# Streamed weights begun ahead of their stage in a four-layer attention and feed-forward kernel

## The chip, the cores and the metric

One Trainium2 chip; the kernel runs on 1 of its cores. The metric is device time in microseconds, the median of 3 runs. A profiled execution gives the trace that all views come from. Engines are named as the profile names them: PE (TensorE, matrix multiply), PEld (its weight loads), DVE (VectorE), ACT (ScalarE), POOL (GpSimd) and SP (SyncE, which here issues nearly all transfers).

## The reference

Sixteen samples x of 256 x 128, each with a context of 1601 x 64, pass through four layers. Every layer is an attention of x over the context and a feed-forward part, each on a layer norm of x and added to x:

```
for l in 0..3:
    x = x + xattn_l(layernorm(x), context)
    x = x + ffn_l(layernorm(x))
```

- Layer 0: causal self-attention plus cross attention, 16 heads of 8; then a mixture of 32 small experts, top 4 (hidden size 1024 in all).
- Layer 1: cross attention, 16 heads of 8; then a convolution with ternary weights and quantised activations.
- Layer 2: two blocks with 16 heads of 32, the first over x itself, the second over the context. Each is attention, a projection (li1), and an inner feed-forward part (norm, li2, gelu, li3). Then 8 experts, top 1.
- Layer 3: cross attention, 16 heads of 8; then 16 experts, top 2, with a shared one (hidden size 1280 in all).

All is float32.

## The kernel before

**The order of work is written out by hand.** A schedule made while the program is built decides in which order each engine gets its instructions; engines then run in that order and wait on semaphores. Two samples ("lanes") are in work at a time. `seq` lists (sample, layer) pairs: both samples' layer 0, both samples' layer 1, and so on, then the next pair.

**The frame is the cross attention over 1601 keys.** It is cut into slabs of 4 heads, 4 slabs to an attention, 256 in all. A slab has 7 steps of two key tiles of 128: scores (`st_ops`, L447), exponentials (`exps`, L462), weighing of values one step later (`weigh`, L473). Beside slab i run the score maxima of slab i + 1 (`Slab.maxima`, L544: matmuls into `bank`, reduced by DVE at L552). After a slab's last step, `normalised` (L485) divides by the sums: for heads of 32 a reciprocal (L502) and a product (L503) on DVE.

**Everything else is coroutines.** `life(b)` (L1033) is a sample's whole path outside the frame; each `yield` in it ends a slot's share. After each step the frame calls `slot()` (L1073) twice, one directly after the other. A slot advances the key line or the value line in turn (keys and values of the coming attention), and then each sample's chain by one `yield`. So what two consecutive steps of a chain do is emitted into the engines' in-order streams with an attention step between them, or with none. When a chain asks for its attention (`attend`, L771) it stands still until its slabs are done. If the next slab's sample isn't that far, `until` (L1094) calls slots with no attention between them. That happens ahead of every l2 cross attention: 12 slots for each sample, and 25 at the very end.

**The chain of l2.** `l2_attn` (L960) calls `mha` (L905) twice. The first, pre `l2_a1`, attends to the sample itself: norm, transpose, `affine_T`, then q, k and v from the streamed `qkv` weights, then `own_attention` (L564). The second, pre `l2_a2`, is the cross attention. Both end alike: load the streamed `li` weights, first `down` (L759; 4 chunks of 128 and a bias row), norm, transpose, `hidden`, gelu, second `down`.

**Streamed weights.** Weights that don't fit for good come through `stream` (L263): a tile of 128 x 1536 from a pool of two buffers (`wst`), and one transfer issued by SP at L266. `ws_room`, a `Room(2)` (L59), counts the free buffers while the program is built: `take` yields until there is one. There are 8 streamed loads a sample: `s_l0f_0` and `_1` in `l0_ffn` (L810), `s_l2_a1_qkv`, `s_l2_a1_li` and `s_l2_a2_li` in `mha`, `s_l3f_0` to `_2` in `l3_ffn` (L997). Each is issued where its stage begins, followed by two or three empty yields.

**SP's queue** is in order too. Besides the streamed loads it holds the context, x, the output, and the spreads (`spread`, L407: 4 transfers for a slab, 16 for a tensor) that place queries and keys of heads of 8 in four row groups. A transfer into a buffer waits for the last reader of that buffer.

Of the kernel before, what the change touches and what calls it, by code (L numbers as in the profile page):

```python
# [20 lines left out]
P = 128  # L21
# [53 lines left out]
def model(ctx: ExitStack, tc: tile.TileContext, d, out):  # L75
# [187 lines left out]
    def stream(n, w):  # L263
# [2 lines left out]
        nc.sync.dma_start(out=t[:, :w], in_=d[n])  # L266
        return t

    def ln(src, tag="z"):

        st = sm.tile([P, 2, 6], F32, tag="st", name=name("st"))
        mv = sm.tile([P, 2, 2], F32, tag="mv", name=name("mv"))
        rs = sm.tile([P, 2], F32, tag="rs", name=name("rs"))
        for q in range(2):
            nc.vector.bn_stats(out=st[:, q, :], in_=src[:, q, :])  # L275
            nc.vector.bn_aggr(out=mv[:, q, :], in_=st[:, q, :])
        nc.vector.tensor_scalar(rs, mv[:, :, 1], EPS, None, ALU.add)  # L277
        nc.gpsimd.tensor_tensor(rs, rs, neghalf[:, 0:2], ALU.pow)  # L278
        yield
        z = tok(tag)  # L280
        for q in range(2):
            nc.vector.tensor_scalar(  # L282
                z[:, q, :], src[:, q, :], mv[:, q, 0:1], rs[:, q : q + 1], ALU.subtract, ALU.mult
            )
        return z
# [141 lines left out]
    class Att:  # L427
# [4 lines left out]
        def __init__(self, dims, q, nk):  # L432
            self.d8 = dims == 8
            self.q, self.nk = q, nk
            self.scale = S8 if self.d8 else S32
            self.k, self.v = {}, {}
            self.o = tok("o") if self.d8 else wide("oT")
            self.done = False

        def value(self, s, t, g, r):  # L440
            if self.nk == T:
# [366 lines left out]
        return residual(x, tok_out([(cols(yT), W["l0_Wp"]), bias_row(0)]))  # L808

    def l0_ffn(x):  # L810
        z = yield from ln(x)
        xz = tok("xz")
        nc.gpsimd.tensor_tensor(xz, x, z, ALU.add)
        zT = yield from to_T(z)
        p = bank()
        mm(p[:32, :T], W["l0f_hash"], zT)
        hT = chan("hT")[:32, :T]
        evac(hT, p[:32, :T])
        yield
        lg = wp.tile([P, 2, 32], F32, tag="lg32", name=name("lg"), bufs=1)  # L820
        evac(lg, tok_out([(cols(hT), W["l0f_keys"])], n=32))
        yield
        gate = wp.tile([P, 2, 32], F32, tag="gate32", name=name("gate"), bufs=1)
        yield from route(lg, 32, 4, gate)
        gT = yield from gates_T(gate, 32)
        o = xz
        for c0 in (0, 4):
            yield from ws_room.take()
            w = stream(f"s_l0f_{c0 // 4}", 1024)
            for _ in range(2):  # L830
                yield
            h = wide("h")
            s = flat(h)
            for i in (0, 512):
                nc.scalar.activation(s[:, i : i + 512], hidden(w, zT, i // T), AF.Silu)
            yield
            for i in (0, 512):
                nc.vector.tensor_tensor(s[:, i : i + 512], expanded(exp32, gT, c0 + i // T), s[:, i : i + 512], ALU.mult)
            yield
            p = down([h], w[:, 512:], 4)  # L840
            ws_room.give()
            n = tok("x")
            nc.vector.scalar_tensor_tensor(n, p, W["l0f_scale"], o, ALU.mult, ALU.add)
            o = n
        return o
# [58 lines left out]

    def mha(x1, pre, cross, r0):  # L905

        z = yield from ln(x1)
        yield
        pz = transposed(z)
        xT = affine_T(pz, pre + "_lnx_g", pre + "_lnx_b", "xT")  # L910
        if cross:
            yield
            q = yield from slabs(W[pre + "_wq"], xT, "q")
            att = Att(32, q, NK)
            yield from attend(att)
        else:
            yT = affine_T(pz, pre + "_lny_g", pre + "_lny_b", "yT")
            yield from own_room.take()
            yield from ws_room.take()
            w = stream("s_" + pre + "_qkv", 1536)  # L920
            for _ in range(3):
                yield
            q = yield from slabs(w[:, :512], xT, "q")
            k = yield from slabs(w[:, 512:1024], yT, "k")
            v = wide("v")
            for t in range(2):
                p = bank()
                mm(p, yT[:, t * P : (t + 1) * P], w[:, 1024:])
                evac(flat(v)[:, t * 512 : (t + 1) * 512], p)
                yield  # L930
            ws_room.give()
            att = Att(32, q, T)
            att.k = {s: k[:, s, :] for s in range(4)}
            att.v = {0: flat(v).rearrange("p (t h e) -> p t h e", t=2, h=H)}
            yield from own_attention(att, False, (ALU.is_gt, 1))
            own_room.give()
        o = att.o
        yield from ws_room.take()
        w = stream("s_" + pre + "_li", 1536)
        for _ in range(3):  # L940
            yield
        p = down([o], w, 4, [bias_row(r0)])
        xo = tok("xo")
        nc.vector.tensor_tensor(xo, p, x1, ALU.add)
        z = yield from ln(xo)
        yield
        zT = affine_T(transposed(z), pre + "_ln3_g", pre + "_ln3_b", "xT")
        yield
        h = wide("h")
        pr = [hidden(w[:, 512:1024], zT, c) for c in (0, 2)]  # L950
        for c in range(4):
            nc.scalar.activation(
                h[:, c, :], pr[c // 2][:, (c % 2) * T : (c % 2 + 1) * T], AF.Gelu, bias=W[pre + "_li2_b"][:, c : c + 1]
            )
        yield
        p = down([h], w[:, 1024:], 4, [bias_row(r0 + 1)])
        ws_room.give()
        return xo, p
# [36 lines left out]
        return residual(x, down([h], flat(W["l2f_W2"]), 2, [(cols(gT), W["l2f_b2"])]))  # L995

    def l3_ffn(x):  # L997
        z = yield from ln(x)
        zT = yield from to_T(z)
        lg = wp.tile([P, 2, 17], F32, tag="lg17", name=name("lg"), bufs=1)  # L1000
        evac(lg, tok_out([(cols(zT), W["l3f_Wg"])], n=17))
        yield
        gate = wp.tile([P, 2, 17], F32, tag="gate17", name=name("gate"), bufs=1)

        sg = sm.tile([P, 2], F32, tag="sg", name=name("sg"), bufs=1)
        nc.scalar.activation(sg, lg[:, :, 16], AF.Exp, scale=-1.0)
        yield from route(lg[:, :, :16], 16, 2, gate[:, :, :16])
        nc.vector.tensor_scalar(sg, sg, 1.0, None, ALU.add)
        nc.vector.reciprocal(gate[:, :, 16], sg)
        gT = yield from gates_T(gate, 17, 32)  # L1010
        for c0, n in ((0, 4), (4, 4), (8, 2)):
            yield from ws_room.take()
            w = stream(f"s_l3f_{c0 // 4}", 3 * n * P)
            for _ in range(2):
                yield
            h = wide("h")
            s = flat(h)
            for i in range(0, n * T, 512):
                nc.scalar.activation(s[:, i : i + 512], hidden(w, zT, i // T), AF.Silu)
            yield  # L1020
            for i in range(0, n * T, 512):
                o = s[:, i : i + 512]
                nc.vector.tensor_tensor(o, hidden(w[:, n * P :], zT, i // T), o, ALU.mult)
            yield
            for i in range(0, n * T, 512):
                o = s[:, i : i + 512]
                nc.vector.tensor_tensor(o, expanded(exp64, gT, c0 + i // T), o, ALU.mult)  # L1027
            yield
            x = residual(x, down([h], w[:, 2 * n * P :], n))
            ws_room.give()  # L1030
        return x
# [17 lines left out]
    ready = {}  # L1049
# [23 lines left out]
    def slot():  # L1073
        begin()
        if later:
            g = later.popleft()
            if advance(g)[0]:
                later.appendleft(g)
        for i, l in enumerate(lines):
            if i == turn[0] % 2:  # L1080
                advance(l)
        turn[0] += 1
        for c in list(chains):
            if c[0] is not None and c[0] in ready:
                if not ready[c[0]].done:
                    continue
                del ready[c[0]]
            alive, att = advance(c[1])
            if att is not None:
                ready[c[0]] = att  # L1090
            if not alive:
                chains.remove(c)
# [10 lines left out]
    def slab(i):  # L1103

        n, s = divmod(i, 4)
        if n >= len(seq):
            return None
        b = seq[n][0]
        until(lambda: b in ready and not ready[b].done and n in k_of and s in k_of[n])
        att = ready[b]  # L1110
        att.k, att.v = k_of[n], v_of.setdefault(n, {})
        slabs_of[i] = Slab(att, s, i % 2)
        return slabs_of[i]

# [8 lines left out]
    with tc.manual_schedule():  # L1123
# [28 lines left out]
        for i in range(4 * len(seq)):  # L1152
            nxt = slab(i + 1)
# [155 lines left out]
```

## Time and profile before

| | |
|---|---|
| median of 3 runs | 11254.35 us (11251.69 to 11277.46) |
| profiled execution, its own time | 11315.87 us |
| its span, first to last instruction | 11313.9 us |
| mean granted TensorE clock | 0.795 |
| busy: PE, DVE, ACT, POOL | 9940.3, 5942.1, 4978.6, 952.6 us |
| DMA queue q1 (SP's), share of 16 engines | 11.4% |
| li loads (`ws<-in_s_l_a_li_dram`) | 32 of 768.0 KB, 4.2 us to landing |
| l0f loads | 32 of 512.0 KB, 5.5 us |
| l3f loads | 32 of 768.0 KB, 6.7 us, and 16 of 384.0 KB |

A line of the timeline gives start, duration, engine, source line, operation, output<-inputs, shape and count; in brackets the idle time of that engine before it, and what ended it. A line of the waits gives who waited for whom, the sum in us, how often, and the longest. Most matrix operations stand under L172, the helper `mm`, so they are told apart by their tiles: `bank<-ws,oT` is the first down of an li stage, `bank<-xT,ws` its hidden layer (or q of the first l2 block), `bank<-ws,h` its second down; `mx<-k,q` are scores of an own attention; `nmp` and `nmT` carry the shift by the maxima. The durations of matmuls overlap, since PE is pipelined.

### The profile page before, as it was taken

What the parts mean: (1) busy time and instruction counts of PE and PEld (TensorE: products, weight loads), DVE (VectorE), ACT (ScalarE), POOL (GpSimd) and SP (SyncE); (2) the same over time, 40 slices, a digit from 0 to 9 for tenths busy, and PEclk for the clock granted to TensorE, in tenths of its full rate; (3) what the DMA queues carried; (4) which work ended last, traced back from release to release, by engine and by line L of the source; (5) the groups of instructions that cost most, each with busy time, mean ns of one, the idle gap of its engine ahead of it and who ended that gap; (6) DMA issues with size and microseconds to landing.
All of it is one profiled execution on the core that took longest, in us unless ns stands there. A gap on an engine that the chain in (4) does not pass through costs nothing.

```text
span 11313.9 us, 204909 instructions
## 1 busy us (share of the span) xinstructions
PE 9940.3 (88%) x86834; PEld 5384.7 (48%) x86874; DVE 5942.1 (53%) x13070; ACT 4978.6 (44%) x6812; POOL 952.6 (8%) x2283
## 2 busy tenths in 40 slices
PE   6989899898998979989798897988989989798898
PEld 3445444454444544445454454544544445454454
DVE  4544555445554455545555454554555545455455
ACT  3433454334543445434454344543444434444344
POOL 2000100001000010000100001000010000100000
PEclk7679777796777977789777896778977689777897
DMA  2100111001110011100111001110011100111011
GB/s 57 36 7 15 35 44 36 7 18 36 40 36 7 18 38 39 36 7 18 42 39 31 7 19 42 37 31 7 20 43 36 31 7 19 43 36 32 7 23 26
DMA packets 158827, 313.09 MB, mean 28 GB/s; under 512 B 65163, under 2 KB 116275, under 8 KB 157910
## 3 DMA queue, kind: packets, MB, share of 16 engines
q1 hardware_dynamic: 154676, 297.83, 11.4%
q8 instruction: 683, 11.19, 0.4%
q14 instruction: 234, 1.92, 0.1%
q0 software_dynamic: 768, 1.48, 0.0%
q10 hardware_dynamic: 2466, 0.68, 0.0%
HBM read 98.31 MB, written 2.10 MB: 9 GB/s over the span
## 4 chain that ended last, share of the span: by engine, by line
PE 73%; DVE 13%; ACT 5%; issue 4%; POOL 3%; SPq 2%; DMA 1%; DVEq 0%; POOLq 0%; ACTq 0%
PE bank L172 58%; PE st L172 10%; DVE mx L552 4%; ACT p L464 3%; DVE nm L579 2%; SPq L411 2%; PE mx L172 1%; PE bank L492 1%; PE bank L298 1%; POOL rs L278 1%; DVE z L282 1%; POOL p L603 1%; DVE st L275 1%; DVE hl L405 1%; ACT y L239 1%
## 5 line engine op out<-in xcount | busy, mean ns | idle before, releaser
L552 DVE TENSOR_REDUCE mx<-bank 128x1 f32<-128x400 f32 (+2 forms) x8192 | 4165.5, 568 | 2382.7 <-PE bank L172 2292.8
L464 ACT ACTIVATE p<-st 128x1024 f32<-128x1024 f32 (+1 forms) x3840 | 3500.6, 963 | 3735.0 <-PE st L172 2376.3
L172 PE MATMUL bank<-k,q 32*128 32x400 f32 (+2 forms) x10240 | 3663.6, 574 | 479.6 <-DVE mx L552 265.8
L172 PEld LDWEIGHTS bank<-k,q 32*128 32x128 f32 x10240 | 1653.0, 216 | 1900.6 <-DVE mx L552 1065.7
L172 PE MATMUL bank<-p,v 128*9 128x256 f32 (+3 forms) x27648 | 2483.3, 472 | 32.5 <-POOL p L603 32.5
L172 PE MATMUL st<-q,k 32*128 32x256 f32 (+1 forms) x18176 | 2011.0, 394 | 156.5 <-DVE nm L579 82.4
L172 PEld LDWEIGHTS st<-q,k 32*128 32x128 f32 (+1 forms) x18176 | 1313.4, 213 | 507.4 <-ACT p L464 174.3
L172 PE MATMUL st<-nmT,ones 32*128 32x512 bf16 (+1 forms) x7680 | 1291.8, 442 | 0.0
L172 PEld LDWEIGHTS bank<-p,v 128*9 128x9 f32 (+3 forms) x27648 | 688.0, 105 | 1243.6 <-issue 988.7
L172 PE MATMUL bank<-p,ones 128*32 128x256 f32 (+1 forms) x7680 | 611.3, 392 | 20.2 <-ACT p L464 20.2
L509 POOL CAST nmp<-nm 128x8 bf16<-128x8 f32 x384 | 83.7, 218 | 6017.6 <-DVE nm L558 4434.6
L579 DVE TENSOR_REDUCE nm<-mx 128x4 f32<-128x1024 f32 x256 | 301.7, 1221 | 317.2 <-PE mx L172 312.5
L172 PEld LDWEIGHTS <-ones 32*128 32x128 bf16 (+1 forms) x7680 | 410.2, 109 | 41.1
L278 POOL TENSOR_TENSOR rs<-rs,neghalf 128x2 f32<-128x2 f32 x240 | 167.6, 698 | 3002.5 <-DVE rs L277 3002.5
L239 ACT COPY v<-bank 128x512 f32<-128x512 f32 (+3 forms) x592 | 228.8, 449 | 372.2 <-PE bank L172 372.2
L172 PEld LDWEIGHTS bank<-p,ones 128*32 128x32 f32 (+1 forms) x7680 | 251.8, 113 | 217.2 <-ACT p L464 39.4
L603 POOL TENSOR_SCALAR_AFFINE_SELECT p<-p 128x1024 f32<-128x1024 f32 x256 | 266.6, 1063 | 841.6 <-PE bank L172 524.1
L502 DVE RECIPROCAL rc<-bank 128x256 f32<-128x256 f32 x128 | 224.7, 1756 | 175.4 <-PE bank L172 171.6
L172 PE MATMUL bank<-ws,h 128*128 128x128 f32 x1664 | 307.0, 351 | 3.2 <-DVE h L1027 0.8
L464 ACT ACT_TABLE_LOAD x141 | 180.9, 1283 | 262.0 <-PE st L172 139.1
L172 PEld LDWEIGHTS bank<-ws,h 128*128 128x128 f32 x1664 | 275.7, 255 | 38.6 <-DVE h L1027 12.5
L492 PE MATMUL bank<-ident,y 128*128 128x128 f32 x512 | 136.3, 360 | 155.1 <-ACT y L239 154.6
(240 smaller groups left out, 7258.1 us busy)
## 6 DMA issues: line engine op xcount, KB each, us to landing
k<-hl SPq DMA_DIRECT2D x768, 200.2 KB, 4.0
q<-hl SPq DMA_DIRECT2D x1024, 32.0 KB, 1.9
ws<-in_s_l_a_li_dram SPq DMA_DIRECT2D x32, 768.0 KB, 4.2
ws<-in_s_l3f_dram SPq DMA_DIRECT2D x32, 768.0 KB, 6.7
ws<-in_s_l0f_dram SPq DMA_DIRECT2D x32, 512.0 KB, 5.5
ws<-in_s_l_a_qkv_dram SPq DMA_DIRECT2D x16, 768.0 KB
k<-hl SPq DMA_DIRECT2D x256, 32.0 KB, 1.9
ws<-in_s_l3f_dram SPq DMA_DIRECT2D x16, 384.0 KB
```

What stands on the lines that cost most here:

```text
L172: nc.tensor.matmul(out=o, lhsT=l, rhs=r, start=start, stop=stop, skip_group_check=free)
L239: nc.scalar.copy(o, i)
L275: nc.vector.bn_stats(out=st[:, q, :], in_=src[:, q, :])
L278: nc.gpsimd.tensor_tensor(rs, rs, neghalf[:, 0:2], ALU.pow)
L282: nc.vector.tensor_scalar(z[:, q, :], src[:, q, :], mv[:, q, 0:1], rs[:, q : q + 1], ALU.subtract, ALU.mult)
L411: nc.sync.dma_start(out=raw(o)[r::4, :], in_=raw(hl[c])[32 * s : 32 * s + 32, :])
L464: nc.scalar.activation(e[:r, :, :n, :], sc[:r, :, :n, :], AF.Exp, scale=att.scale)
L492: nc.tensor.transpose(t[:, q * P : (q + 1) * P], y[:, q * P : (q + 1) * P], ident)
L502: nc.vector.reciprocal(rc, av[:, 1, :])
L552: nc.vector.tensor_reduce(self.mx[:, q, g, c : c + 1], p[:, : k1 - k0], AX.X, ALU.max)
L579: nc.vector.tensor_reduce(o, sc[hp], AX.X, ALU.max, negate=True)
L603: nc.gpsimd.affine_select(out=e, in_=e, pattern=[[0, 2], [sign * P, 2], [-sign, T]], compare_op=op, fill=0.0, base=0, channel_multiplier=sign,
```

## The change

A load is begun ahead of its stage if a buffer is free at that point; otherwise it is made at the stage as before, now with four empty yields. Where it was begun ahead, the stage has no empty yield. The points: at the norm of `l0_ffn`, `l3_ffn` and the first `mha`; one group ahead within `l0_ffn` and `l3_ffn`; after the v projection for the first `li`; and for the second `li` once the attention's last slab has had its maxima begun (`began` reaches 3). So that `mha` can watch `began`, a chain that waits for its attention is now advanced in every slot; it still goes on only when the attention is done.

```diff
+    def early(n, w):
+        if not ws_room.n:
+            return None
+        ws_room.n -= 1
+        return stream(n, w)
+
+    def arrived(t, n, w):
+        if t is None:
+            yield from ws_room.take()
+            t = stream(n, w)
+            for _ in range(4):
+                yield
+        return t
...
+            self.began = 0
...
     def l0_ffn(x):
+        nxt = early("s_l0f_0", 1024)
         z = yield from ln(x)
...
         for c0 in (0, 4):
-            yield from ws_room.take()
-            w = stream(f"s_l0f_{c0 // 4}", 1024)
-            for _ in range(2):
-                yield
+            w = yield from arrived(nxt, f"s_l0f_{c0 // 4}", 1024)
+            nxt = early("s_l0f_1", 1024) if c0 == 0 else None
...
     def mha(x1, pre, cross, r0):
+        nxt = None if cross else early("s_" + pre + "_qkv", 1536)
         z = yield from ln(x1)
...
-            yield from attend(att)
+            wait = attend(att)
+            yield next(wait)
+            while att.began < 3:
+                yield
+            nxt = early("s_" + pre + "_li", 1536)
+            yield from wait
         else:
...
-            yield from ws_room.take()
-            w = stream("s_" + pre + "_qkv", 1536)
-            for _ in range(3):
-                yield
+            w = yield from arrived(nxt, "s_" + pre + "_qkv", 1536)
...
             ws_room.give()
+            nxt = early("s_" + pre + "_li", 1536)
...
         o = att.o
-        yield from ws_room.take()
-        w = stream("s_" + pre + "_li", 1536)
-        for _ in range(3):
-            yield
+        w = yield from arrived(nxt, "s_" + pre + "_li", 1536)
...
     def l3_ffn(x):
+        nxt = early("s_l3f_0", 1536)
         z = yield from ln(x)
...
         for c0, n in ((0, 4), (4, 4), (8, 2)):
-            yield from ws_room.take()
-            w = stream(f"s_l3f_{c0 // 4}", 3 * n * P)
-            for _ in range(2):
-                yield
+            w = yield from arrived(nxt, f"s_l3f_{c0 // 4}", 3 * n * P)
+            nxt = early(f"s_l3f_{c0 // 4 + 1}", 768 if c0 else 1536) if c0 < 8 else None
...
         for c in list(chains):
-            if c[0] is not None and c[0] in ready:
-                if not ready[c[0]].done:
-                    continue
+            if c[0] in ready and ready[c[0]].done:
                 del ready[c[0]]
             alive, att = advance(c[1])
...
         att.k, att.v = k_of[n], v_of.setdefault(n, {})
+        att.began = s
```

## The prediction

> **What bounds the kernel now.** I read four views, from wide to narrow: the page, the PE's own waits, the timeline at the longest of them, and a table of stretches.
>
> The page first: the lines of busy time and of the chain.
>
> ```profile
> span 11313.9 us, 204909 instructions
> PE 9940.3 (88%) x86834; PEld 5384.7 (48%) x86874; DVE 5942.1 (53%) x13070; ACT 4978.6 (44%) x6812; POOL 952.6 (8%) x2283
> PE 73%; DVE 13%; ACT 5%; issue 4%; POOL 3%; SPq 2%; DMA 1%; DVEq 0%; POOLq 0%; ACTq 0%
> ```
>
> PE is busy for 88% and holds 73% of the chain; DMA holds 1%. Earlier loads can win only where PE stands still: at most 11313.9 - 9940.3 = 1374 us, and in fact only what of it hangs on the streamed weights. The PE's own waits say how much that is (us, times, longest):
>
> ```profile
> PE bank L172 <- DVE mx L552: 265.8, 316, 5.4
> PE bank L298 <- DVE z L282: 151.7, 39, 11.8
> PE bank L172 <- DMA ws<-in_s_l_a_li_dram: 81.0, 7, 13.4
> ```
>
> Only one stream is ever waited for: the li weights, 7 times, 81.0 us (0.7%). The l0f, l3f and qkv streams do not appear, so loading them earlier is worth nothing directly. The timeline at one of the seven, SP and then PE (start, duration):
>
> ```profile
> 3990.58 10.04 SPq L411 DMA_DIRECT2D q<-hl  x16
> 4000.72 13.90 SPq L411 DMA_DIRECT2D k<-hl  x20
> 4014.67 1.04 SPq L266 DMA_DIRECT2D ws<-in_s_l_a_li_dram  x1
> 4015.81 11.25 SPq L411 DMA_DIRECT2D q<-hl  x16
> ```
>
> ```profile
> 4007.91 0.48 PE L172 MATMUL bank<-rows,ones 1*128 1x128 f32 x2
> 4021.52 2.08 PE L172 MATMUL bank<-ws,oT 128*128 128x128 f32 x8 [13.12 <-DMA ws<-in_s_l_a_li_dram]
> ```
>
> The load isn't slow: 6.85 us from issue to use. It is issued late, behind 36 small spreads of about 0.65 us each in SP's order. This is the second sample of a pair in its second (cross) block, where the next pair's l0 spreads come in. The other 25 li loads are issued well ahead already, because SP runs ahead of PE.
>
> The second place is the gap ahead of the l2 cross attention. There the emission loop calls slots with no attention between them:
>
> ```profile
> 3519.51 1.05 PE L172 MATMUL bank<-p,v 128*9 128x256 f32 x16
> 3522.85 0.29 PE L172 MATMUL bank<-ident,nmp 128*128 128x128 bf16 x2 [2.29 <-POOL nmp L512]
> ...
> 3532.26 0.49 PE L298 MATMUL bank<-ident,z 128*128 128x128 f32 x2 [1.12 <-DVE z L282]
> 3533.41 2.76 PE L172 MATMUL bank<-xT,ws 128*128 128x256 f32 x8 [0.66 <-ACT xT L311]
> ...
> 3548.38 0.73 PE L298 MATMUL bank<-ident,z 128*128 128x128 f32 x2 [6.76 <-DVE z L282]
> 3549.77 3.78 PE L172 MATMUL bank<-xT,w_l_a_wq 128*128 128x256 f32 x8 [0.65 <-ACT xT L311]
> 3553.48 1.04 PE L172 MATMUL bank<-k,q 32*128 32x402 f32 x2
> ```
>
> From 3519.1 to 3553.5 PE does only the li chain: 34.4 us for a pair's first sample, 30.7 to 32.7 for its second.
>
> **The change part by part.** All sums are against the profiled execution (11315.87 us), which is 0.55% above the median of 11254.35.
>
> *What moves.* The slots can be counted from the loops before anything runs. The gap has 12 of them in each sample; with the change it has 6, since 3 yields go at qkv and 3 at li. All slots together go from 3825 to 3723: 16 x 6, and 6 at the end. No operation is added or removed. In the changed SP order, the second sample's last li load stands right behind an earlier l3 key spread, two slabs ahead of its use, and no longer behind the 36 spreads.
>
> *The li wait, 7 x 11.6 = 81.0 us.* It goes. What is late next: the next pair's own attention (mx<-k,q) needs k spreads that SP issues until 4014.6, and PE now arrives 13 us sooner. Its first score came at 4005.64, so slab 0 is there in time, and slabs 1 to 3 are issued by about 4011. Ends: 0 (the spreads take over the whole wait) and 81; I take 10 of each 11.6, so **-70**, since most of the spreads are already issued.
>
> *The clock after that wait.* The li matmuls took 4.80 us after the wait against 2.66 for the same group at full clock elsewhere. I take 2 us for each of the 7: **-14** (ends 0 and 28).
>
> *The gap.* Six slots fewer are not half of 34 us, and this is where I chose. The last two slots of the attention step before the gap were empty and are now filled with the hidden matmuls and second down, which nothing covers there either. Truly put under attention are the first down, its norm and the transpose: 3524.02 to 3533.41 = 9.4 us, plus the 2.29 us that PE waited for the shift (its reduction stood behind a 1.76 us reciprocal that now comes earlier). The same stretch in the second sample, at a higher clock, is 7.3 + 1.1. What is put under attention still costs PE its time: down 2.66, transpose 0.5, the key matmuls inside it 1.0 and a new in-order wait. Down now comes one slot after the last slab's division (1.76 + 0.42 us on DVE; 2.3 us from last weigh matmul to oT), with no attention between. A bias row, three of four chunks and sometimes a value tile come first, so 1.5 of it stays. Together 5.7; at half clock 2.5 more. First sample 11.7 - 7.2 = 4.5, second 8.4 - 5.7 = 2.7: 3.6 x 16 = **-58** (ends: 0, and half the gap, 16 x 16 = 260).
>
> *New in-order waits elsewhere.* PE takes matmuls in order, so the attention step behind pays. In the cross block, li's down now follows the division in the same slot: 1 us each for the nine without a DMA wait before, **+9** (ends 0 and 2.3 x 16 = 37). At qkv, q's matmuls follow the transpose in the same slot: ACT's xT costs 0.66 us in the row at 3533.41 and up to 2.6 behind an exponential pair of 1.94 us; 1.3 x 16 = **+21** (ends 10 and 42).
>
> *At nothing:* l0f and l3f loads (no row waits for them; cover: SP is slabs ahead; without it, 6.7 us a load); the tail, where the third l3f load waits for the first buffer as before and the 6 slots gone were empty; an early load behind a buffer still being read, which holds SP only until PE reaches that point, with the spreads emitted later behind it (without that, one slab's wait, 22 to 44 us).
>
> **A rule against the trace.** The rows first, of the gap and of the slab after it; the columns are stretch, its length, busy of PE, PEld, DVE, ACT, POOL, clock, DMA, GB/s.
>
> ```profile
> 3519.10:3553.50 34.40, 22.92 (x98) 15.29 (x97) 9.22 (x29) 7.90 (x15) 3.70 (x8) 0.62 0.07 24
> 3559.00:3595.00 36.00, 35.75 (x227) 16.93 (x231) 14.84 (x30) 11.23 (x14) 0.87 (x4) 0.50 0.00 1
> ```
>
> PE is busy for 35.75 of 36 us and the clock stays at 0.50. The Trainium skill (TensorE: Matmul & The Clock Gate, Part 1: The HAM clock gate) says the opposite: about 3.4 us of sustained activity brings full clock back. By the rule this slab would be at full clock after one window and no gain lies there. By the row, about 16 us are lost here in each pair (36 against some 20 at full clock), and a gap that ends otherwise could free 8 x 16 = 128 us, or put other slabs into that state. Nothing in the trace says which way it falls, so the sum has 0, and the range takes it in.
>
> Sum: -70 - 14 - 58 + 9 + 21 = -112 us of 11315.87, that is 11204 profiled; scaled by 0.995, 11254 - 111 = **11143 us** (-1.0%).
>
> **The rivals.**
> - *As summed* (0.56): 11090 to 11200.
> - *More than summed* (0.19): the gap really halves (-260 in place of -58), or the half-clock slab goes (-128). For it: the slab repeats in every pair behind this gap. Against it: half of the freed slots stand uncovered. About 11015 with the slab, 10940 with the gap.
> - *The wait only changes its name* (0.18): with the spreads still serial on SP, own attention or a bank waits for them in place of li, and of -84 only some 20 are left: 112 - 64 = 48, so 11206; with the gap's part gone too it is -20 + 30 = +10, 11264. For it: SP is busy without a break from 3990 to 4027, and PE stood 5 us at 3996.8 for other work of this knot. Most of it is within 0.3%.
> - *Slower* (0.07): the merged slots. At 48 places (32 downs, 16 qkv) PE now stands in order ahead of a short chain on DVE or ACT. Without these waits the gains are 81 + 14 + 58 + 24 (the 1.5 us taken off the gap) = 177; from 177 / 48 = 3.7 us a place the change loses. I take 1 to 1.5; with the whole 2.3 us and as much again until DVE's reductions (265.8 us waited for already) have caught up it is 4.6, so 48 x 4.6 - 177 = +44: 11298.
>
> **How the numbers follow.** A measurement of this kernel can tell about 0.3% (34 us) from no change. Below 11220 lie the first two cases and a part of the third: faster 0.79; same 0.15; slower 0.06. The range runs from the half-clock slab freed (11020) to the wait renamed with little left (11245).
>
> **What would show it.** Right: the li row is gone from PE's waits and no k or q row of like size comes; the last st matmul to the first maxima of the l2 attention falls from 34 and 31 us to some 23; new PE waits for oT (L503) and xT of 1 to 2 us. Wrong: a DMA k<-hl row of tens of us; a gap of 17 us (I underrated) or over 28; the slab behind the gap at a clock of 1.0, or other slabs fallen to 0.5; oT waits near 4 us.

## The result and the profile after

The changed kernel takes 11099.24 us (median of 4 executions, 11084.67 to 11147.29) against 11265.90 us of the kernel before on the same chip (11251.69 to 11295.38): ratio 0.9857, 95% interval [0.9825, 0.9888]. Set against the 11254 us of the prediction, that is -161 us where -111 was forecast; the forecast of 11143 us was 44 us too high (50 by the change itself: the kernel before was 12 us slower this time). The profiled execution took 11147.29 us at a mean granted clock of 0.803 (before: 11315.87 us at 0.795). Both profiled executions are slower than their medians, by 48 and 50 us, so their difference, 169 us, is close to the 167 us between the medians.

The same lines of the page, for the kernel after:

```profile
span 11145.6 us, 204895 instructions
PE 9898.0 (89%) x86834; PEld 5378.0 (48%) x86874; DVE 5941.6 (53%) x13070; ACT 4979.3 (45%) x6812; POOL 953.4 (9%) x2283
PE 72%; DVE 14%; ACT 6%; issue 4%; POOL 3%; SPq 1%; DMA 0%; DVEq 0%; POOLq 0%; ACTq 0%
```

PE has the same 86834 matmuls. It is busy 42 us less and idle 126 us less (11145.6 - 9898.0 = 1248 against 1374): the gain is mostly idle time, and partly the same matmuls at a higher clock. PE's own waits (us, times, longest):

```profile
PE bank L172 <- DVE mx L569: 265.4, 320, 5.2
PE bank L314 <- DVE z L298: 81.9, 20, 11.7
PE mx L172 <- DVE nm L596: 78.9, 84, 14.8
PE bank L172 <- DVE oT L520: 45.7, 56, 1.1
```

The row for the li weights (81.0 us) has gone, and no row for spreads of that size has come. The wait for the norm, z, fell by 70 us (151.7 to 81.9). Of the waits that have grown, the two largest are 45.7 us for oT, which is new, and 78.9 us for the shift reduction (48.9 before). PE's wait for ACT's copy of the values v, which the prediction didn't name, fell from 43.7 to 10.1 us. The DVE maxima are unchanged at 265 us. The gap ahead of the l2 cross attention, same pair as in the prediction (timeline, PE: start, duration):

```profile
3485.66 1.90 PE L172 MATMUL bank<-p,v 128*9 128x256 f32 x16
3487.49 0.39 PE L172 MATMUL bank<-ident,nmp 128*128 128x128 bf16 x2
3487.67 2.03 PE L172 MATMUL bank<-xT,ws 128*128 128x256 f32 x8
...
3493.14 2.33 PE L172 MATMUL bank<-ctxT,w_l_a_wkv 64*128 64x448 f32 x8
3500.07 0.66 PE L314 MATMUL bank<-ident,z 128*128 128x128 f32 x2 [4.59 <-DVE z L298]
3501.38 3.71 PE L172 MATMUL bank<-xT,w_l_a_wq 128*128 128x256 f32 x8 [0.66 <-ACT xT L327]
3505.03 0.61 PE L172 MATMUL bank<-k,q 32*128 32x402 f32 x2
```

First down (ws,oT), its norm and its transpose no longer stand in the gap, the shift (nmp) isn't waited for, and the final z is waited for 4.59 us in place of 6.76. All 16 gaps, from the last st matmul of one attention to the first of the next, sum to 316.2 us (19.7 and 19.9 each) against 531.0 (34.2 and mostly 32.3). The prediction had expected some 23.

The stretches show one thing more: the gap, and then the slab behind it in the same pair and in the next one. Columns as in the prediction (stretch, length, PE, PEld, DVE, ACT, POOL, clock, DMA, GB/s):

```profile
3485.30:3505.00 19.70, 14.44 (x72) 8.71 (x64) 4.92 (x18) 7.55 (x15) 2.13 (x3) 0.76 0.12 41
3508.00:3536.00 28.00, 25.75 (x270) 12.71 (x269) 17.63 (x37) 14.90 (x18) 0.88 (x4) 1.00 0.01 1
4875.00:4898.00 23.00, 21.14 (x133) 10.81 (x129) 10.42 (x21) 8.96 (x11) 0.00 (x0) 0.57 0.00 1
```

The slab behind the gap fell to half clock in all 8 pairs before. Now it stays at 1.00 in three pairs; in the other five it has full clock for its first 3.41 or 6.83 us and then half (0.58 or 0.65 over 22 us). The slab at full clock puts 270 matmuls through in 28 us, the other one 133 in 23 us, with PE busy for 92% of both. This was the part that the prediction had set at 0 with 128 us in the range.

### The profile page after: what moved, and what is told of

Read it like the earlier page. It is cut to its first block, busy times and chain, and to the rows that moved or that the text cites. A ratio compares the mean times of both kernels' runs of the same rounds, so it can differ in the third digit from the quotient of the medians.

```text
span 11145.6 us, 204895 instructions
## 1 busy us (share of the span) xinstructions
PE 9898.0 (89%) x86834; PEld 5378.0 (48%) x86874; DVE 5941.6 (53%) x13070; ACT 4979.3 (45%) x6812; POOL 953.4 (9%) x2283
## 4 chain that ended last, share of the span: by engine, by line
PE 72%; DVE 14%; ACT 6%; issue 4%; POOL 3%; SPq 1%; DMA 0%; DVEq 0%; POOLq 0%; ACTq 0%
PE bank L172 57%; PE st L172 10%; DVE mx L569 5%; ACT p L481 3%; DVE nm L596 2%; PE mx L172 1%; PE bank L509 1%; SPq L427 1%; PE bank L314 1%; DVE rc L519 1%; POOL p L620 1%; POOL rs L294 1%; DVE z L298 1%; DVE st L291 1%; DVE hl L421 1%
## 5 line engine op out<-in xcount | busy, mean ns | idle before, releaser
L172 PE MATMUL bank<-k,q 32*128 32x400 f32 (+2 forms) x10240 | 3617.9, 568 | 447.1 <-DVE mx L569 265.4
L172 PEld LDWEIGHTS bank<-k,q 32*128 32x128 f32 x10240 | 1630.7, 215 | 1932.4 <-DVE mx L569 1129.3
L172 PE MATMUL bank<-p,v 128*9 128x256 f32 (+3 forms) x27648 | 2450.0, 467 | 12.6 <-POOL p L620 12.6
L172 PE MATMUL st<-q,k 32*128 32x256 f32 (+1 forms) x18176 | 2015.5, 393 | 151.7 <-ACT p L481 91.8
L509 PE MATMUL bank<-ident,y 128*128 128x128 f32 x512 | 136.3, 357 | 188.7 <-ACT y L239 174.6
L172 PEld LDWEIGHTS bank<-ws,h 128*128 128x128 f32 x1664 | 265.0, 243 | 35.1 <-issue 17.1
L512 DVE RECIPROCAL rc<-bank 128x8 f32<-128x8 f32 x256 | 53.0, 207 | 416.5 <-PE bank L509 416.5
```

Of the source, the lines that this page charges most:

```text
L172: nc.tensor.matmul(out=o, lhsT=l, rhs=r, start=start, stop=stop, skip_group_check=free)
L509: nc.tensor.transpose(t[:, q * P : (q + 1) * P], y[:, q * P : (q + 1) * P], ident)
```

## The experiments

All ratios are to the kernel before on the same chip, with the 95% interval. One per cent is 113 us. They fall into three questions: loads or slots, which stage, and what the clock does. A slab's length is taken from one reduction into `nm` on DVE (L558 in the kernel before, one for each slab) to the next, a gap's from the last st matmul of one attention to the first of the next. Sums over slabs and gaps are of the profiled executions.

**Loads ahead, all empty yields kept.** `arrived` gets the number of empty slots to leave, whether or not the load is there.

```
-    def arrived(t, n, w):
+    def arrived(t, n, w, gap):
         if t is None:
             yield from ws_room.take()
             t = stream(n, w)
-            for _ in range(4):
-                yield
+        for _ in range(gap):
+            yield
```

> The loads are begun ahead as in the changed kernel, but every stage keeps its 2 or 3 empty yields, so the slots are those of before (12 in each l2 gap). Theory (two separate gains: the load order at seven li loads, and the slots taken out ahead of the l2 cross attention): only the li wait of 81 us and some 10 us of half clock after it go, gaps stay at 34 and 32 us; 75 to 95 us faster than before, ratio 0.992 to 0.9935. Rival 1 (the loads carry it all): 150 to 170 us faster, ratio 0.985 to 0.987. Rival 2 (the slots carry it all, the li wait returns as a wait for spreads): within 20 us of before.

Measured: 11172.93 us, 0.9936 [0.9919, 0.9954]: 72 us faster (52 to 91). The li row is gone, the gaps are the old ones (sum 529.9 us), and the slab that held the wait went from 78.4 to 64.4 us in the median. So the moved loads alone give what the prediction's first two terms said, with no spread waited for instead.

**The yields removed, no load ahead.** From before, the empty `yield` loop behind each streamed load is taken out, in all four places:

```
         w = stream("s_" + pre + "_li", 1536)
-        for _ in range(3):
-            yield
```

> No load is begun ahead; the empty yields after each streamed load are taken out (6 slots in each l2 gap, as in the changed kernel). Theory: the gaps fall to about 20 us as with the whole change; the first block's li and the qkv loads are not waited for, since SP runs ahead of PE; but the second block's li load is issued where it was and used three slots sooner, so PE waits for it 7 times at 11 to 18 us and 8 to 9 times at some 4 to 7 us, 120 to 180 us in all against 81. In sum 50 to 110 us faster than before, ratio 0.990 to 0.9955. Rival 1 (the loads carry it all): not faster than before, rather slower. Rival 2 (the slots carry it all): as the changed kernel, ratio 0.985 to 0.987.

Measured: 11329.86 us, 1.0065 [1.0048, 1.0081]: slower, a miss. The gaps fell as expected, to the same 19.7 and 19.9 us (sum 316.8). But PE's waits of this kernel have this row:

```profile
PE bank L172 <- DMA ws<-in_s_l_a_li_dram: 208.9, 16, 26.8
```

Sixteen waits of 13 us in place of seven of 11.6: the empty slots had been the cover of the load's flight. That alone doesn't make the kernel slower, since the gaps are 214 us shorter and this wait is 128 us longer. The feed-forward stages' yields, which are out here too, cost 79 us by themselves (below); the rest isn't assigned. The two halves of the change need each other. Loads ahead are worth 0.64% with the yields kept, and 0.9857 / 1.0065, some 2.1%, with them gone.

**The attention's part alone** (`mha` as changed, the feed-forward stages as before):

```
     def l3_ffn(x):
-        nxt = early("s_l3f_0", 1536)
...
-            w = yield from arrived(nxt, f"s_l3f_{c0 // 4}", 3 * n * P)
-            nxt = early(f"s_l3f_{c0 // 4 + 1}", 768 if c0 else 1536) if c0 < 8 else None
+            yield from ws_room.take()
+            w = stream(f"s_l3f_{c0 // 4}", 3 * n * P)
+            for _ in range(2):
+                yield
```

and the same in `l0_ffn`.

> Only the part of the change in mha (qkv and both li loads); l0f and l3f load at their stage with two empty yields as before. Theory by the stage sums of the two traces (the l3 and l0 feed-forward parts, pulled forward into fewer slots, cost some 44 us in the slabs beside them): 25 to 45 us faster than the changed kernel, ratio to before 0.981 to 0.984. As the record had it (those parts at nothing): the same as the changed kernel within 15 us, ratio 0.985 to 0.987. Rival (they gain by themselves): slower than the changed kernel by 20 us or more.

Measured: 11020.73 us, 0.9801 [0.9778, 0.9823], better than the whole change. The slab behind the gap is at full clock in 6 of 8 pairs.

**The feed-forward part alone**, the complement of that edit (`mha` as before, `l0_ffn` and `l3_ffn` as changed):

> Only the part of the change in l0_ffn and l3_ffn; mha as before, with its late li load and 12 slots in each gap. Theory by the stage sums: 20 to 45 us slower than before, ratio 1.002 to 1.004. As the record had it (at nothing): within 15 us of before. Rival (they gain by themselves): faster by 20 us or more. The li wait of some 81 us should still be in the trace.

Measured: 11339.07 us, 1.0070 [1.0057, 1.0083]: 79 us slower, more than expected. Here is where part of the gain is given back.

**Which of the two.** Only `l3_ffn` changed, then only `l0_ffn`:

> Only the part of the change in l3_ffn; all else as before. The feed-forward part as a whole cost 0.7% (79 us). Theory (empty yields gone make PE, ACT and DVE run a chain of matmuls, SiLU and products back to back beside the fullest slabs, where the next pair's own attention and context come in): l3f carries most of it, 40 to 70 us slower than before, ratio 1.0035 to 1.006. Rival (the cost comes with the number of groups that lose their yields, 3 for l3f against 2 for l0f, wherever they are): 45 to 50 us for l3f and 30 to 35 for l0f. Rival 2 (it is a matter of both together, a shift of phase): each alone within 15 us.

> Only the part of the change in l0_ffn; all else as before. Theory (l3f carries most): 10 to 30 us slower, ratio 1.001 to 1.003. Rival (by the number of groups): 30 to 35 us slower. Rival 2 (both together): within 15 us.

Measured: l3f alone 11359.72 us, 1.0065 [1.0045, 1.0086]; l0f alone 11266.63 us, 0.9980 [0.9969, 0.9991], a small gain where a small loss was expected. The third layer's feed-forward carries the whole cost, 73 us or 4.6 us in each of its 16 runs. The first slab of layer 3's second sample, as one stretch of before and then of this kernel, shows part of it:

```profile
4176.30:4253.30 77.00, 64.44 (x453) 34.53 (x460) 35.04 (x78) 36.56 (x57) 13.93 (x32) 0.67 0.14 35
```

```profile
4195.40:4278.90 83.50, 69.05 (x476) 38.00 (x479) 37.68 (x82) 37.85 (x58) 13.97 (x32) 0.68 0.16 42
```

With six slots fewer in the stage, 23 more matmuls fall into this slab (453 to 476), at a clock of 0.67 and 0.68. It takes 6.5 us longer, of which PE is idle 1.9 us; over the 8 pairs the same slab sums to +57 us, and the one after it gives back 16. Two of PE's waits tell more of it:

```profile
PE bank L509 <- ACT y L239: 174.0, 201, 2.4
PE bank L509 <- ACT h L1035: 13.6, 7, 2.1
```

The first was 154.6 us before; the second, a bank that this stage's SiLU (L1035) still reads, has no row before. Both stand in the whole change too (174.6 and 14.0 us), and not in the attention's part alone.

**l3f with one of its two yields kept:**

```
             w = yield from arrived(nxt, f"s_l3f_{c0 // 4}", 3 * n * P)
+            yield
             nxt = early(f"s_l3f_{c0 // 4 + 1}", 768 if c0 else 1536) if c0 < 8 else None
```

> Only the part of the change in l3_ffn, but with one empty yield left of the two at each group; all else as before. With none left it cost 0.65%, with both left (loads ahead all the same) nothing. Theory (without an empty yield one group's down and the next group's hidden layer are emitted in one slot, a block of matmuls in which attention gets nothing, and SiLU holds the banks): one yield ends that, ratio 0.999 to 1.002. Rival (the cost comes from where the chain stands against the slabs, so it goes with the number of slots taken out): half the cost or so, ratio 1.002 to 1.005.

Measured: 11347.57 us, 1.0043 [1.0026, 1.0061]. One yield, which already parts the down of a group from the next hidden block, brings back about a third of the cost; two thirds remain with half of the slots taken, and the two intervals overlap. The waits of the merged block are gone: 159.2 us for y, no row for the SiLU, and PE idle for 1369 us in all against 1439 with none of the yields and 1374 before. So the merged block is a part and not the whole, and what remains stands in no wait of PE. That the cost goes with the number of slots taken out fits it, and isn't proved by one point. The slab of the stretch above stands in between as well (79.5 us in the median, of 77.0 and 83.7).

**The gap once more: shorter still.** The attention's part, and in `quantised` (layer 1) the yield behind each half is taken out too, so that two slots are left in the gap:

```
             nc.vector.tensor_scalar(o[:, q, :], o[:, q, :], -128.0, am[:, q, 2:3], ALU.max, ALU.mult)
-            yield
```

> The attention part of the change alone, and ahead of the l2 gap four more slots are taken out: the yields after each half of the quantisation in l1_ffn, which has only DVE work. 2 slots are left in each gap. Theory (the gap is what the chain has left to do when the last attention step is emitted): the gap falls from 19.8 to 8 to 11 us, PE's idle time of 5 us in it and its half clock go, the slab after it is at full clock in all pairs; 60 to 120 us faster than the attention part alone, ratio to before 0.9695 to 0.975. Rival (the gain came from the loads, and the gap is now PE work that must be done somewhere): within 30 us of the attention part alone, 0.978 to 0.983.

Measured: 11131.36 us, 0.9873 [0.9849, 0.9896]: a miss, some 0.7% slower than the attention's part alone, though the gaps fell to 11.8 and 9.0 us (sum 165.2) and the slab with the gap from 46.5 to 33.3 us. PE's waits have this row, which was 41.9 us in the attention's part alone:

```profile
PE bank L172 <- POOL nmp L529: 142.6, 58, 4.7
```

What left the gap came back in earlier slabs. Summed over the 8 pairs, against the attention's part alone: the slab with the first gap fell by 127 us, and the three slabs ahead of it grew by 94, 21 and 69; the slab with the second gap fell by 87, the three ahead of it changed by +73, +24 and -34, and the one behind it grew by 59. Why these slabs can't take the work in isn't settled beyond that row: the shift that POOL makes is waited for 101 us more.

**Yields kept in the cross block only.** The attention's part, with the li load ahead but three empty slots left ahead of the first down in the cross block:

```
         w = yield from arrived(nxt, "s_" + pre + "_li", 1536)
+        for _ in range(3 if cross else 0):
+            yield
         p = down([o], w, 4, [bias_row(r0)])
```

> The attention part of the change alone, with its loads ahead, but the second (cross) block keeps 3 empty yields ahead of its first down. No gap lies behind these yields, and without them PE stands 0.5 to 1.1 us at the division of the last slab (PE's waits for oT: 45 us in all, about half of them here). Theory: 10 to 25 us faster than the attention part alone, ratio to before 0.978 to 0.979, and half the oT waits gone. Rival (fewer slots are better everywhere): slower than the attention part alone by 10 us or more.

Measured: 10994.19 us, 0.9745 [0.9722, 0.9768], 0.56% below the attention's part alone and more than expected. PE's wait for oT fell as expected, from 45.1 us (56 times) to 26.2 (32 times), but it isn't the gain: the wait for ACT's copy of v came back (11.1 to 49.0 us), and PE is idle for 1229 us in all against 1182. What fell is PE's busy time, 9826.9 to 9763.5 us, at a mean clock of 0.818 in place of 0.812. The slab behind the gap is at full clock in all 8 pairs.

**The clock alone.** Kernel before, with work added: in `l2_attn`, between the residual sum and the last norm of the gap, four matmuls of 128 x 512 whose result nothing reads.

```
         nc.vector.tensor_tensor(x2, x2, xo, ALU.add)
+        for _ in range(4):
+            mm(bank(), ident, convw[:, 0, :])
         z = yield from ln(x2)
```

> The kernel before, with all its slots and late loads; added are 4 matmuls of 128x512 that nobody reads, in each l2 gap right behind the second down, where PE stood idle for 6.8 us (twice a pair for each sample: once in the first block's gap only, since the code runs once a sample). They are work on top, 64 matmuls of about 1 to 2 us. Theory (the slab behind the first sample's gap stays at half clock because PE stood idle in the gap; 8 to 10 us each pair): that slab, 35 us long before, falls to about 27 in most pairs, and the kernel is 30 to 70 us faster in spite of the added work, ratio 0.994 to 0.9975. Rival (the clock of that slab has another cause, and the gap's length is all that counts): no slab changes; same or up to 30 us slower, ratio 1.000 to 1.0025.

Measured: 11137.08 us, 0.9869 [0.9837, 0.9901]: adding 64 useless matmuls makes the kernel 1.3% faster. The gap and the slab behind it, same pair as before:

```profile
3445.70:3477.90 32.20, 25.70 (x106) 15.95 (x98) 9.19 (x29) 7.89 (x15) 3.69 (x8) 0.73 0.08 25
3477.90:3501.00 23.10, 21.13 (x207) 10.53 (x207) 14.83 (x31) 12.31 (x14) 0.00 (x0) 1.00 0.01 1
```

The gap is even 2 us shorter, its clock 0.73 in place of 0.62, and the slab takes 23.1 us at full clock, in all 8 pairs, where it took 35.1. Per pair the slab with its gap fell from 69.3 to 55.3 us, 111 us in all; the slab with the second sample's gap gave about 23 more. So the slab needs no much shorter gap for this. Whether it needs one that PE doesn't leave idle is another matter: the next kernel's is idle.

**The clock and the gap apart.** The version with the cross block's yields, and three empty slots kept at qkv too (9 slots in the gap):

```
             w = yield from arrived(nxt, "s_" + pre + "_qkv", 1536)
+            for _ in range(3):
+                yield
             q = yield from slabs(w[:, :512], xT, "q")
```

> The best so far (attention part, loads ahead, 3 empty yields kept in the cross block), but the 3 empty yields at qkv are kept too, so that 9 slots are left in the l2 gap and not 6. Theory (the gap holds what the chain still has to do, and what is put under attention is nearly free): the first down, its norm and the transpose are back in the gap, which is some 28 to 32 us for the first sample and 26 to 30 for the second; half or more of the gain from the slots is lost, ratio 0.982 to 0.989. Rival (only the clock behind the gap counts): ratio stays at 0.974 to 0.977 where that slab keeps its full clock.

Measured: 11101.34 us, 0.9839 [0.9811, 0.9868], within the expected range, but not by the expected road. The gap did not shrink (mostly 35.4 and 30.4 us, sum 525.1), which is a miss; it is what the prediction's remark on the last two slots of the attention step would give, since the three slots taken out at li only bring the work to where nothing covers it either. Yet the slab behind it is at full clock in 7 of 8 pairs, and at 0.75 in the eighth. The gap's end and the slab, first as timeline and then as stretches:

```profile
2080.36 0.66 PE L314 MATMUL bank<-ident,z 128*128 128x128 f32 x2 [6.85 <-DVE z L298]
2081.67 3.78 PE L172 MATMUL bank<-xT,w_l_a_wq 128*128 128x256 f32 x8 [0.66 <-ACT xT L327]
```

```profile
2050.00:2085.40 35.40, 23.83 (x96) 15.51 (x88) 9.18 (x29) 7.91 (x15) 3.70 (x8) 0.57 0.07 22
2085.40:2108.00 22.60, 20.80 (x206) 10.36 (x205) 14.21 (x29) 11.82 (x13) 0.00 (x0) 1.00 0.01 2
```

The wait for z (6.85 us) and the q matmuls at half clock (3.78 us) are the ones of before to a tenth of a microsecond, and the slab goes the other way. So the last idle stretch can't be what decides alone; the last section has what does differ. Against the same version without these three slots (gaps of 317.0 us in sum) the time goes from 0.9745 to 0.9839: about 1%, 106 us, is what 208 us of gap are worth by themselves, with the same clock behind the gap in all but one pair.

**The parts put together.** The cross block's version and the changed `l0_ffn`:

> The best so far (attention part, loads ahead, 3 empty yields kept in the cross block) together with the l0_ffn part, which alone measured 0.2% faster; l3_ffn as before. Theory (the parts add): ratio to before 0.9715 to 0.974. Rival (they share the same slack, or the l0f part moves the phase of later work): 0.9745 to 0.978.

Measured: 10980.54 us, 0.9726 [0.9696, 0.9756], the fastest of all: the change without its l3f part and with three empty slots left in the cross block. The interval overlaps that of the version without l0f.

## Why the prediction came out 44 us high

The sign and the bulk were right, but the closeness is partly luck: two errors cancel, a gap term that was too small and the l3f stage, set at nothing. In order of its steps, with the kernels that isolate them:

| step | predicted, us | measured, us | from |
|---|---|---|---|
| li wait and clock after it | -70 - 14 = -84 | -72 | loads ahead alone |
| gap and the slab behind it, with oT and qkv stalls | -58 + 9 + 21 = -28 | about -153 | attention alone / loads ahead alone = 0.9864 |
| l0f and l3f | 0 | +79 | feed-forward alone |
| sum | -112 | -146 | (whole change: -161 [-197, -126]) |

*What moves* was right: 12 slots in a gap became 6 and the total 3723, and the late li load lost its place behind the 36 spreads.

*The li wait and the clock after it* were right: the slab concerned fell by 14.0 us where 10 of the 11.6 us of wait and 2 for the clock were taken. The rival that the wait changes its name has fallen: nothing waits for the spreads instead.

*The gap* is the step that failed, in size; the mechanism is there. It was given 11.7 and 8.4 us taken out, less 7.2 and 5.7 for the work put elsewhere. (By its own working the 7.2 should be 5.7 + 2.5 = 8.2, and the term -50.) Measured are 14.5 and 12.4 taken out: the final wait for z shrank too (6.76 to 4.59 us in the first sample), which the prediction had left as it was. Part of it is paid back around the gap. The three slabs ahead of the one with the gap, where the work went, take 159.6 us together in the first sample against 160.2 with the loads alone, and 181.3 against 175.5 in the second (means over the pairs), and the slabs behind the gaps are some 2 and 3 us longer where the clock is the same. Over all eight slabs of the two attentions the changed kernel needs 162 us less than the one with the loads alone. Some 30 of this are the clock's (next paragraph), so about 130 are left of 214 us of gap. The nine-slot kernel gives 106 of 208. So the term was 106 to 130 where 58 were taken: the price of the work put elsewhere, 12.9 us a pair, was about right (some 11 to 13), and what comes out of the gap was too low, 20 us a pair against 27.

*The half-clock slab*, weighed between rule and row and then set at 0, is the second part of it. About 10 us a pair came free (56.7 to 46.5 us with the gap), in 3 of 8 pairs of the changed kernel's profile: some 30 us. In the attention's part alone it is 6 of 8, with the cross block's yields 8 of 8. The filled gap shows the size: 111 us, 2 of the 14 us a pair from the gap itself. The row was right that a busy slab at half clock does not soon free itself. But it was read as a slab that never gets full clock, and its stretch starts just too late to show otherwise: full clock is there for 3.41 us ahead of it (last section). So the question was what makes the slab lose it, and any other length of the gap was a reason to give the 128 us some weight in the sum; it had none.

*oT in the cross block*, +9, named the wait (19 us of it go when those yields are given back), but not the cost: the yields were worth 0.56%, about 63 us, while PE's waits in sum got no shorter. Some 20 us of it are the two further slabs at full clock. The two profiled executions are only 17 us apart, so the rest can't be placed.

*qkv*, +21, can't be seen: PE's wait for xT is 21.0 us after, as much as with the loads alone. Whether the attention step behind q pays in another form wasn't isolated.

*At nothing* failed for l3f. The prediction named SP and the transfers as cover, and no transfer is waited for; but it priced only the load that moves, not the empty slots that go with it. Six slots out of each of its 16 runs cost 73 us. About a third of it is the merged-slot mechanism of the slower rival, in a stage where the rival hadn't put it: the waits for y and behind the SiLU, some 33 us, go when one yield of two is kept, and 25 us come back. At the attention, where the rival had put it, the gain was far larger than the loss. What the other two thirds are stays open: the trace shows more matmuls in a slab at two thirds of the clock, and not what they push out. l0f, with the same edit, gains 23 us, so it isn't the edit as such.

## What to carry to other kernels

An empty slot ahead of a load's use is two things, cover for the load and spacing for the in-order engines. Before taking it out, price both: loads ahead alone gave 0.6%, yields out alone lost 0.65%, both 1.4%, and both only where the spacing isn't needed 2.7%. And where a busy stretch behind an idle one runs at half clock, test it with a few filler matmuls before any scheduling work: the test takes two lines and was worth 1.3% here. It shows that time is to be had, not why: a filler also moves all that follows against the steps of the clock (below).

## What was not expected of the hardware

**A slab that gets full clock and loses it.** The slab behind the first gap gets full clock within 2.4 us of its start in every kernel here, and then keeps it or loses it. The slab of the prediction's row, in the kernel before, with its first microseconds:

```profile
3555.00:3558.30 3.30, 2.66 (x22) 0.97 (x17) 2.60 (x5) 2.59 (x3) 0.00 (x0) 1.00 0.00 0
3558.40:3595.00 36.60, 35.75 (x227) 16.93 (x231) 14.84 (x30) 11.83 (x15) 0.87 (x4) 0.50 0.00 1
```

It came back only after 37.55 us, though PE was busy. That some 3.4 us of sustained activity bring back full clock (the Trainium skill, TensorE: Matmul & The Clock Gate, Part 1: The HAM clock gate) is not what the second row shows: 36 us of it did not.

**Where the slab starts between two steps of the clock.** Whether the slab keeps full clock goes neither by the gap's length (kept behind first gaps of 11.8, 19.7, 32.2 and 35.4 us, lost behind 19.7 and 34.2) nor by the wait just ahead (6.85 us and kept, 6.76 us and lost). The granted clock in all these traces is 0.5 or 1.0, and each stretch at one of them lasts a multiple of 3.41 us. So it changes in steps of that length, and a slab can start anywhere between two. Here are two pairs of the changed kernel, with a gap of 19.7 us in both: the first 6.5 us of the slab, and the 27.9 us behind.

```profile
2112.50:2119.00 6.50, 5.03 (x53) 2.73 (x52) 3.21 (x8) 4.07 (x5) 0.00 (x0) 1.00 0.01 3
2119.10:2147.00 27.90, 27.90 (x164) 13.19 (x159) 12.93 (x26) 9.69 (x10) 0.00 (x0) 0.50 0.00 1
3505.10:3511.60 6.50, 5.02 (x52) 2.74 (x52) 3.21 (x8) 4.07 (x5) 0.00 (x0) 1.00 0.00 0
3511.70:3539.60 27.90, 26.60 (x273) 13.74 (x271) 16.78 (x35) 15.00 (x20) 0.88 (x4) 1.00 0.01 1
```

The first 6.5 us are alike, but in the first pair the clock rose 0.21 us ahead of the slab's first score, in the second 0.15 us ahead. The same holds over the 104 first gaps of all kernels but the one with two slots. Where a step fell between 0.18 us ahead of the first score and 0.39 us behind it, the slab kept full clock (43 of 43). Elsewhere it lost it after 3.41 or 6.83 us (61 of 61), mostly for 27 to 38 us. In the kernel with two slots, whose slabs hold other work, full clock stayed with a step 0.46 to 0.77 us ahead. This was found in the traces afterwards, no kernel moved the slab on purpose, and why it must start near a step stays open.

So the filled gap can be read in two ways: it keeps PE from standing idle, and it moves the slab to within 0.1 us of a step (before, the step came 1.5 us behind its start). The pairs of one kernel often meet the steps at the same place (before: 1.47 to 1.57 us in all 8), so 8 of 8 is not eight independent trials. Filling the gap of the fastest version wasn't tried.

**More work can take less time.** The gap with 64 more matmuls in it was 34 us shorter in sum (497.1 against 531.0), and ran at a higher clock (0.73 in place of 0.62 in the rows shown).
